# A four-layer graph network in one kernel: the first chunk of its last layer done alone, and the scaling of layer 2's outputs pinned one chunk ahead

## Chip, cores and metric

The kernel runs on one core of a Trainium2 chip. The metric is the device time of one execution in microseconds (us). Engines are named as the profile names them: PE (matrix multiplications, with PEld for its weight loads), DVE (vector), ACT (scalar, activation functions), POOL (general, elementwise here) and SP (issues DMA transfers). Each has a queue of its own and works through it in order; semaphores tie the queues together.

## What is computed

Four graph layers are applied to x, 128 graphs of 64 nodes with 256 features, each with a residual connection: x = x + layer(relu(layernorm(x))). All arithmetic is in fp32. Only the end of layer 2 and layer 3 matter here:

```python
# layer 2
h = relu(batchnorm(agg @ W1.T + b1, g1, be1))      # agg = A_hat @ relu(layernorm(x))
out = batchnorm(h @ W2.T + b2, g2, be2)            # mean and variance over all 8192 tokens
x = x + out
# layer 3
h = relu(layernorm(x))                             # mean and variance over the 256 features of a token
Wh = h @ W
e = leaky_relu(s1[:, :, None] + s2[:, None, :])    # s1 = Wh @ a1, s2 = Wh @ a2
e = where(adj == 0, -inf, e)
x = x + softmax(e) @ Wh
```

The batch normalization that ends layer 2 needs all tokens before the first can be scaled. So layer 3 can start only when layer 2 has been through the last token: there is a seam between the two.

## The kernel before

The 8192 tokens are worked in 16 chunks of 512, a chunk being four token tiles of 128. Layer 2 leaves its raw outputs in SBUF with features on the partitions, `hs[n][0]`, and `fold2.of` (line 1544) turns the collected statistics into a scale and a shift per feature. The residual x of each chunk is loaded by `fetch` (line 1568) into `hs[n][1]` with tokens on the partitions.

Layer 3 then takes each chunk through these steps:

- `second_norm(n)` (line 1572). It makes `o`, the scaled outputs of layer 2, in a buffer of the pool `xin2`, which has four (for chunk 0 one half on DVE, line 1579, and one on ACT, line 1582; for all others both halves on POOL, line 1587). Eight PE transposes with the identity (line 1594) bring it into a pair of PSUM banks, DVE adds it to the residual (line 1596), and takes mean and variance of each of the four token tiles (lines 1600 and 1601). The roots, (variance + 1e-5) to the power -0.5, and the negative product with the mean are four small POOL operations (lines 1603 to 1607). The normalized chunk `h` is four operations of 128x256, on ACT for chunk 0 (line 1615) and on POOL for all others (line 1611).
- `features(n)` (line 1619): eight transposes back (line 1626) and a relu on ACT into `hT` (line 1629).
- `project3(n, tiles)` (line 1635): per token tile two matrix multiplications of 257 columns, copied to `wh` by ACT (line 1650). The multiplications are recorded under the helper's line 50, as are those of the scores and values.
- `dense_scores(n)` (line 1652): the scores, their leaky relu, mask and maximum on DVE (lines 1662 to 1671), exponentials on ACT (line 1674), a reciprocal on DVE (line 1677).
- `turn(n)` (line 1680): four transposes of the exponentials (line 1685), copied by DVE and then ACT into a block-diagonal `field` (line 1689).
- `dense_values(n)` (line 1693): four multiplications, then scale and residual add on DVE (line 1700), and the store of the chunk (line 1708).

The loop at line 1712 writes these out for staggered chunks: in step n, `second_norm(n+2)`, `features(n+1)`, `project3(n)`, `turn(n-1)`, `dense_scores(n)`, `dense_values(n-1)`. This order is only the order of priority. A scheduler fills each engine's queue when the kernel is built, and may put an instruction ahead of earlier ones if it deems its inputs ready sooner. In the built program before, POOL's queue opens layer 3 with ten scalings, those of chunks 1 to 5, ahead of the roots of chunk 0; from then on the scaling of a chunk stands four to five chunks ahead of its use. The helper `late(ins)` (line 71) takes that freedom away: it pins an instruction behind everything written before it for the same engine.

## Time and profile before

| | us |
|---|---|
| median of three runs | 2114.04 |
| lowest and highest of them | 2113.0, 2115.65 |
| the profiled execution: its time | 2112.7 |
| the profiled execution: its span, first to last instruction | 2110.9 |
| last matrix multiplication of layer 2 ends | about 1946.9 |
| first and last transposes L1594 of layer 3 start | 1950.8, 2075.9 |
| last operation on DVE ends, the last store is issued | 2106.7 |

Times inside the profile count from the start of the span. A profile has several views. The totals give each engine's busy time. The view by stretches gives it for parts of the span, with the granted clock of PE (1.00 is full). The chain of waits goes back from the last instruction, at each step to what released it. The timeline lists instructions in order of time. A line such as `h<-pair,h 128x1024` names the tile written and those read.

### The profile page before, as it was taken

What the parts mean: (1) busy time and instruction counts of PE and PEld (TensorE: products, weight loads), DVE (VectorE), ACT (ScalarE), POOL (GpSimd) and SP (SyncE); (2) the same over time, 40 slices, a digit from 0 to 9 for tenths busy, and PEclk for the clock granted to TensorE, in tenths of its full rate; (3) what the DMA queues carried; (4) which work ended last, traced back from release to release, by engine and by line L of the source; (5) the groups of instructions that cost most, each with busy time, mean ns of one, the idle gap of its engine ahead of it and who ended that gap; (6) DMA issues with size and microseconds to landing.
All of it is one profiled execution on the core that took longest, in us unless ns stands there. A gap on an engine that the chain in (4) does not pass through costs nothing.

```text
span 2110.9 us, 25487 instructions
## 1 busy us (share of the span) xinstructions
PE 2028.9 (96%) x9444; PEld 1348.2 (64%) x9444; DVE 1352.1 (64%) x2453; ACT 1186.4 (56%) x2264; POOL 309.1 (15%) x432
## 2 busy tenths in 40 slices
PE   8999999999999999999999998999999989999898
PEld 6776488766688746886668884333334665434686
DVE  8764665564655577556546555576676767786676
ACT  4354766654655467656456554565565356591444
POOL 3000000100200020002001002113312420000662
PEclk9999999999999999999999999999999999999899
DMA  9221000100100340001000006113234751022012
GB/s 315 88 95 50 0 21 1 41 0 1 40 1 1 120 159 20 1 1 40 1 11 30 1 22 203 60 41 104 67 90 131 230 189 60 0 70 90 30 61 70
DMA packets 94444, 135.06 MB, mean 64 GB/s; under 512 B 6384, under 2 KB 82032, under 8 KB 92144
## 3 DMA queue, kind: packets, MB, share of 16 engines
q1 hardware_dynamic: 87600, 109.11, 15.5%
q0 software_dynamic: 6112, 24.12, 3.8%
q8 instruction: 74, 1.21, 0.2%
q10 hardware_dynamic: 608, 0.20, 0.1%
q14 instruction: 50, 0.41, 0.1%
HBM read 87.28 MB, written 46.14 MB: 63 GB/s over the span
## 4 chain that ended last, share of the span: by engine, by line
PE 81%; ACT 6%; DVE 6%; issue 4%; DMA 2%; POOL 1%; SPq 0%; ACTq 0%; POOLq 0%; DVEq 0%
PE pa L641 24%; PE bank L50 20%; PE pc L641 12%; PE pair L50 6%; PE pb L641 6%; PE pa L1341 5%; PE pc L1341 2%; ACT gate L669 2%; PE bank L1132 1%; PE pb L1341 1%; ACT gate L721 1%; PE pair L1626 1%; DMA xo<-xa 1%; PE pair L1594 1%; DVE lstm_c L720 1%
## 5 line engine op out<-in xcount | busy, mean ns | idle before, releaser
L641 PE MATMUL pa<-xop,sih 128*128 128x256 f32 (+2 forms) x1056 | 346.6, 417 | 11.8 <-ACT gate L689 10.1
L669 ACT ACTIVATE gate<-gate,bias 128x256 f32<-128x256 f32 (+2 forms) x368 | 246.9, 678 | 181.0 <-DVE gate L685 97.4
L641 PEld LDWEIGHTS pa<-xop,sih 128*128 128x128 f32 x1056 | 198.5, 190 | 85.5 <-issue 20.9
L641 PE MATMUL pc<-xop,wih 128*128 128x256 f32 (+2 forms) x736 | 251.1, 423 | 0.0
L641 PE MATMUL pa<-lstm_h,shh 128*128 128x256 f32 (+1 forms) x672 | 212.7, 398 | 0.0
L963 DVE SCALAR_TENSOR_TENSOR lr<-lr 128x1024 f32<-128x1024 f32 x128 | 152.0, 1218 | 85.4 <-ACT lr L962 85.2
L685 DVE TENSOR_TENSOR gate<-pb,gate 128x256 f32<-128x256 f32 (+2 forms) x184 | 87.5, 475 | 162.1 <-PE pb L641 126.0
L641 PEld LDWEIGHTS pc<-xop,wih 128*128 128x128 f32 x736 | 139.8, 190 | 51.2 <-issue 22.5
L699 DVE TENSOR_TENSOR gate<-pc,gate 128x256 f32<-128x256 f32 (+2 forms) x184 | 87.4, 475 | 119.2 <-PE pc L641 117.7
L641 PEld LDWEIGHTS pa<-lstm_h,shh 128*128 128x128 f32 x672 | 127.7, 190 | 30.2
L962 ACT COPY lr<-pair 128x1024 f32<-128x1024 f32 x128 | 125.0, 1015 | 34.3 <-PE pair L50 34.3
L641 PE MATMUL pc<-lstm_h,whh 128*128 128x256 f32 (+1 forms) x448 | 141.8, 398 | 0.0
L684 ACT COPY gate<-pa 128x256 f32<-128x256 f32 (+2 forms) x184 | 76.9, 418 | 104.3 <-PE pa L641 103.6
L669 ACT ACTIVATE gate<-pa,bias 128x256 f32<-128x256 f32 (+2 forms) x184 | 94.8, 515 | 71.1 <-PE pa L641 70.1
L50 PE MATMUL pair<-sd_hot,xq 64*128 64x512 f32 x512 | 134.4, 622 | 0.3 <-ACT lr L962 0.3
L50 PE MATMUL bank<-wlv,hT 128*128 128x512 f32 x256 | 122.8, 611 | 7.0 <-ACT hT L154 7.0
L694 DVE TENSOR_TENSOR gate<-pa,gate 128x256 f32<-128x256 f32 (+2 forms) x184 | 87.4, 475 | 35.3 <-PE pa L641 33.1
L641 PE MATMUL pa<-xop,wih 128*128 128x256 f32 (+1 forms) x320 | 101.8, 400 | 5.4 <-ACT xop L622 3.1
L432 POOL TENSOR_TENSOR sih<-wih 128x512 f32<-128x512 f32 x8 | 10.8, 1350 | 632.2 <-DMA wih<-in_WihT 440.7
L641 PE MATMUL pb<-xop,wih 128*128 128x256 f32 (+1 forms) x320 | 100.5, 398 | 0.0
L641 PEld LDWEIGHTS pc<-lstm_h,whh 128*128 128x128 f32 x448 | 85.1, 190 | 20.1
L50 PEld LDWEIGHTS bank<-wlv,hT 128*128 128x128 f32 x256 | 44.8, 189 | 81.9 <-issue 62.1
(321 smaller groups left out, 3844.2 us busy)
## 6 DMA issues: line engine op xcount, KB each, us to landing
field<-sd_hot SPq DMA_DIRECT2D x8, 1152.0 KB, 10.4
wih<-in_WihT SPq DMA_DIRECT2D x8, 1024.0 KB, 5.0
xres<-in_x SPq DMA_DIRECT2D x16, 512.0 KB, 5.3
xa<-xres POOLq DMA_DIRECT2D x16, 512.0 KB, 4.6
xin<-xb SPq DMA_DIRECT2D x16, 512.0 KB, 3.9
h<-xb SPq DMA_DIRECT2D x16, 512.0 KB, 3.8
out_x<-h SPq DMA_DIRECT2D x16, 512.0 KB, 2.9
xin<-in_x SPq DMA_DIRECT2D x15, 512.0 KB, 5.9
```

Source lines behind the costliest of these rows:

```text
L50: nc.tensor.matmul(o, lhsT, rhs, start=start, stop=stop)
L641: ins = nc.tensor.matmul(p[:, : self.N], weights[kind, self.phase](k, q), x[k], start=first_ and kind == "ih", stop=kind == "hh" or not se ...
L669: nc.scalar.activation(out, in_, AF.Tanh if q == 2 else AF.Sigmoid, bias=bias[:, self.w - 1, 2 * q + j : 2 * q + j + 1],)
L684: nc.scalar.copy(blk[0, 0], pa[:, :N])
L685: nc.vector.tensor_tensor(blk[0, 0], pb[:, :N], blk[0, 0], ALU.add)
L694: nc.vector.tensor_tensor(blk[1, 1], pa[:, :N], blk[1, 1], ALU.add)
L699: nc.vector.tensor_tensor(blk[1, 0], pc[:, :N], blk[1, 0], ALU.add)
L720: nc.vector.tensor_tensor(c_, i_, g_, ALU.mult)
L721: nc.scalar.activation(g_, c_, AF.Tanh)
L962: nc.scalar.copy(lr, p)
L963: nc.vector.scalar_tensor_tensor(lr, lr, 0.2, lr, ALU.mult, ALU.max)
L1341: ins = nc.tensor.matmul(p, lhs[k], x[k], start=first_, stop=last_one, skip_group_check=True)
```

## The change

The first chunk gets a function of its own, `first_norm`, which works in two pairs of token tiles: it scales halves of 256 columns on DVE and ACT, adds and normalizes pair by pair, takes its roots with ACT's Sqrt and a reciprocal on DVE, and uses single PSUM banks. Chunk 1 also takes its roots on ACT, and two of its four `h` tiles are made there. The scaling `o` moves out of `second_norm` into `scale_o`, which is pinned with `late` and called for chunk n+3 after `second_norm(n+2)`. Much of chunks 0 to 2 is pinned too. Step 0 of the loop has an order of its own. The store of the last chunk is issued in two halves, the first after its second token tile. PE, DVE and ACT do the same arithmetic on the same sizes otherwise. In the changed file `second_norm`'s transposes are line 1669, its add 1674, its sums 1678 and 1679, the scalings on POOL 1657, the roots on POOL 1688 to 1691, `h` on POOL 1695; in `first_norm` the add is 1602, the root 1609, `h` 1618, the transposes back 1634.

The built program has this order on POOL: scalings of chunks 1 and 2, two `h` tiles of chunk 1, then roots of 2, `h` of 2, scalings of 3, roots of 3, `h` of 3, scalings of 4, and so on in this alternation to chunk 15.

```diff
+        def first_norm():
+            xt, v = xts[0], hs[0][0]
+            o = os3[0]
...
+            for ip in range(2):
+                r = slice(ip * 256, (ip + 1) * 256)
+                late(nc.vector.tensor_scalar(
+                    o[:, 0, r], v[:, 0, r], scale2[:, 0:1], shift2[:, 0:1], ALU.mult, ALU.add
+                ))
+                late(nc.scalar.activation(
+                    o[:, 1, r], v[:, 1, r], AF.Identity, bias=shift2[:, 1:2], scale=scale2[:, 1:2]
+                ))
+            def add(ip):
+                p = bank()
...
+                flat = xt[:, 2 * ip : 2 * ip + 2, :].rearrange("p i d -> p (i d)")
+                late(nc.vector.tensor_tensor(flat, p, flat, ALU.add))
+
+            def sums(ip):
+                i2 = slice(2 * ip, 2 * ip + 2)
+                for i in (2 * ip, 2 * ip + 1):
+                    late(nc.vector.bn_stats(st[:, i, :], xt[:, i, :]))
+                    late(nc.vector.bn_aggr(mv[:, i, :], st[:, i, :]))
+                late(nc.scalar.activation(rs[:, i2], mv[:, i2, 1], AF.Sqrt, bias=eps))
+
+            def root(ip):
+                i2 = slice(2 * ip, 2 * ip + 2)
+                late(nc.vector.reciprocal(rs[:, i2], rs[:, i2]))
+                late(nc.vector.scalar_tensor_tensor(
+                    nm[:, i2], mv[:, i2, 0], -1.0, rs[:, i2], ALU.mult, ALU.mult
+                ))
+                for i in (2 * ip, 2 * ip + 1):
+                    late(nc.scalar.activation(
+                        h[:, i, :], xt[:, i, :], AF.Identity, bias=nm[:, i : i + 1], scale=rs[:, i : i + 1]
+                    ))
+
+            add(0)
+            sums(0)
+            add(1)
+            root(0)
+            sums(1)
+            root(1)
+            yield
...
+        def scale_o(n):
+            half = (0, 1) if n % 2 == 0 else (1, 0)
+            o = os3[n] = xin2.tile([P, 2, CHUNK], F32, tag="xin2", name="o")
+            v = hs[n][0]
+            for c in range(2 if n else 0):
+                late(nc.gpsimd.tensor_scalar(
+                    o[:, c, :], v[:, half[c], :], scale2[:, c : c + 1], shift2[:, c : c + 1], ALU.mult, ALU.add
+                ))
+
         def second_norm(n):
...
-            o = xin2.tile([P, 2, CHUNK], F32, tag="xin2", name="o")
...
-            else:
-                for c in range(2):
-                    nc.gpsimd.tensor_scalar(
-                        o[:, c, :], v[:, half[c], :], scale2[:, c : c + 1], shift2[:, c : c + 1], ALU.mult, ALU.add
-                    )
+            o = os3.pop(n)
...
             rs = stat.tile([P, 4], F32, tag="ln_rs", name="ln_rs")
-            nc.gpsimd.tensor_scalar(rs, mv[:, :, 1], 1e-5, None, ALU.add)
-            nc.gpsimd.tensor_tensor(rs, rs, half_power, ALU.pow)
+            yield
             nm = stat.tile([P, 4], F32, tag="ln_nm", name="ln_nm")
...
+            if n == 1:
+                keep(nc.scalar.activation(rs, mv[:, :, 1], AF.Sqrt, bias=eps))
+                keep(nc.vector.reciprocal(rs, rs))
+                keep(nc.vector.scalar_tensor_tensor(nm, mv[:, :, 0], -1.0, rs, ALU.mult, ALU.mult))
+            else:
+                nc.gpsimd.tensor_scalar(rs, mv[:, :, 1], 1e-5, None, ALU.add)
+                nc.gpsimd.tensor_tensor(rs, rs, half_power, ALU.pow)
...
             for i in range(4):
-                if n:
+                if n > 1 or i > 1:
...
-            nc.sync.dma_start(out=token_tiles(out, n), in_=xt)
+                if n == NCH - 1 and i % 2:
+                    nc.sync.dma_start(
+                        out=token_tiles(out, n)[:, i - 1 : i + 1, :], in_=xt[:, i - 1 : i + 1, :]
+                    )
+            if n < NCH - 1:
+                nc.sync.dma_start(out=token_tiles(out, n), in_=xt)
...
-        for n in range(-2, NCH + 1):
+        for n in range(3):
+            scale_o(n)
+        start = first_norm()
+        next(start)
+        second = second_norm(1)
+        next(second)
+        for _ in start:
+            pass
+        project3(0, (0, 1))
+        for _ in second:
+            pass
+        for n in range(NCH + 1):
             if 4 <= n + 4 < NCH:
                 fetch(n + 4)
             if n + 2 < NCH:
-                second_norm(n + 2)
-            if 0 <= n + 1 < NCH:
+                for _ in second_norm(n + 2):
+                    pass
+            if n + 3 < NCH:
+                scale_o(n + 3)
+            if n == 0:
+                project3(0, (2, 3))
+                dense_scores(0)
+                features(1)
+                continue
+            if n + 1 < NCH:
                 features(n + 1)
```

More of the change, by code (lines that the diff above doesn't have):

```diff
@@ L1570, in fetch @@
             nc.sync.dma_start(out=xts[n], in_=token_tiles(xb[n]))
+        def first_norm():
+            xt, v = xts[0], hs[0][0]
+            o = os3[0]
+            st = stat.tile([P, 4, 6], F32, tag="ln_st", name="ln_st")
+            mv = stat.tile([P, 4, 2], F32, tag="ln_mv", name="ln_mv")
+            rs = stat.tile([P, 4], F32, tag="ln_rs", name="ln_rs")
+            nm = stat.tile([P, 4], F32, tag="ln_nm", name="ln_nm")
+            h = norms[0] = as_tokens(v)
+            hT = t2.tile([P, 2, CHUNK], F32, tag="aggT2", name="hT3")
+            hT3[0] = hT
+            for ip in range(2):
[8 more added lines that the diff above has]
+                p = bank()
+                for i in range(2):
+                    for c in range(2):
+                        k = (2 * ip + i) * P
+                        ins = nc.tensor.transpose(
+                            p[:, (2 * i + c) * P : (2 * i + c + 1) * P], o[:, c, k : k + P], ident
+                        )
+                        if i + c == 0:
+                            late(ins)
+                flat = xt[:, 2 * ip : 2 * ip + 2, :].rearrange("p i d -> p (i d)")
[23 more added lines that the diff above has]
+            yield
+            norms.pop(0)
+            for ip in range(2):
+                p = bank()
+                for i in range(2):
+                    for c in range(2):
+                        ins = nc.tensor.transpose(
+                            p[:, (2 * i + c) * P : (2 * i + c + 1) * P],
+                            h[:, 2 * ip + i, c * P : (c + 1) * P],
+                            ident,
+                        )
+                        if i + c == 0:
+                            late(ins)
+                late(nc.scalar.activation(
+                    hT[:, :, ip * 256 : (ip + 1) * 256].rearrange("p c (i t) -> p i c t", i=2),
+                    p.rearrange("p (i c t) -> p i c t", i=2, c=2),
+                    AF.Relu,
+                ))
+                yield
@@ L1572, in second_norm @@
+        os3 = {}
+        def scale_o(n):
[5 more added lines that the diff above has]
+                    o[:, c, :], v[:, half[c], :], scale2[:, c : c + 1], shift2[:, c : c + 1], ALU.mult, ALU.add
+                ))
         def second_norm(n):
             xt, v = xts[n], hs[n][0]
-            half = (0, 1) if n % 2 == 0 else (1, 0)
@@ L1577, in second_norm @@
-            o = xin2.tile([P, 2, CHUNK], F32, tag="xin2", name="o")
-            if n == 0:
-                nc.vector.tensor_scalar(
-                    o[:, 0, :], v[:, half[0], :], scale2[:, 0:1], shift2[:, 0:1], ALU.mult, ALU.add
-                )
-                nc.scalar.activation(
-                    o[:, 1, :], v[:, half[1], :], AF.Identity, bias=shift2[:, 1:2], scale=scale2[:, 1:2]
-                )
-            else:
-                for c in range(2):
-                    nc.gpsimd.tensor_scalar(
-                        o[:, c, :], v[:, half[c], :], scale2[:, c : c + 1], shift2[:, c : c + 1], ALU.mult, ALU.add
-                    )
+            o = os3.pop(n)
@@ L1593, in second_norm @@
                     k = (i % 2 * 2 + c) * P
-                    nc.tensor.transpose(p[:, i // 2, k : k + P], o[:, c, i * P : (i + 1) * P], ident)
+                    ins = nc.tensor.transpose(p[:, i // 2, k : k + P], o[:, c, i * P : (i + 1) * P], ident)
+                    if n < 3 and i + c == 0:
+                        late(ins)
             flat = xt.rearrange("p i d -> p (i d)")
-            nc.vector.tensor_tensor(flat, p.rearrange("p b d -> p (b d)"), flat, ALU.add)
+            keep = late if n < 3 else lambda ins: ins
+            keep(nc.vector.tensor_tensor(flat, p.rearrange("p b d -> p (b d)"), flat, ALU.add))
             st = stat.tile([P, 4, 6], F32, tag="ln_st", name="ln_st")
@@ L1599, in second_norm @@
             for i in range(4):
-                nc.vector.bn_stats(st[:, i, :], xt[:, i, :])
-                nc.vector.bn_aggr(mv[:, i, :], st[:, i, :])
+                keep(nc.vector.bn_stats(st[:, i, :], xt[:, i, :]))
+                keep(nc.vector.bn_aggr(mv[:, i, :], st[:, i, :]))
             rs = stat.tile([P, 4], F32, tag="ln_rs", name="ln_rs")
-            nc.gpsimd.tensor_scalar(rs, mv[:, :, 1], 1e-5, None, ALU.add)
-            nc.gpsimd.tensor_tensor(rs, rs, half_power, ALU.pow)
+            yield
             nm = stat.tile([P, 4], F32, tag="ln_nm", name="ln_nm")
-            nc.gpsimd.tensor_tensor(nm, mv[:, :, 0], rs, ALU.mult)
-            nc.gpsimd.tensor_scalar(nm, nm, -1.0, None, ALU.mult)
+            if n == 1:
[5 more added lines that the diff above has]
+                nc.gpsimd.tensor_tensor(rs, rs, half_power, ALU.pow)
+                nc.gpsimd.tensor_tensor(nm, mv[:, :, 0], rs, ALU.mult)
+                nc.gpsimd.tensor_scalar(nm, nm, -1.0, None, ALU.mult)
             h = norms[n] = as_tokens(v)
             for i in range(4):
-                if n:
+                if n > 1 or i > 1:
                     nc.gpsimd.tensor_scalar(
@@ L1707, in dense_values @@
                 )
-            nc.sync.dma_start(out=token_tiles(out, n), in_=xt)
+                if n == NCH - 1 and i % 2:
+                    nc.sync.dma_start(
+                        out=token_tiles(out, n)[:, i - 1 : i + 1, :], in_=xt[:, i - 1 : i + 1, :]
+                    )
+            if n < NCH - 1:
+                nc.sync.dma_start(out=token_tiles(out, n), in_=xt)
         for n in range(4):
             fetch(n)
-        for n in range(-2, NCH + 1):
+        for n in range(3):
[10 more added lines that the diff above has]
+        for n in range(NCH + 1):
             if 4 <= n + 4 < NCH:
```

## The prediction

> **What bounds the kernel now.** I read the engines' totals first, then the busy time by stage, the chain of waits from the end of layer 2 on, a steady stretch of layer 3 in order of time, and last the granted TensorE clock.

> ```profile
> PE 2028.9 (96%) x9444; PEld 1348.2 (64%) x9444; DVE 1352.1 (64%) x2453; ACT 1186.4 (56%) x2264; POOL 309.1 (15%) x432
> ```
> ```profile
> 1946.00:1972.00 26.00, 15.87 (x78) 12.49 (x77) 14.11 (x42) 6.75 (x14) 18.68 (x32) 0.67 0.08 27
> ...
> 1980.00:2077.00 97.00, 97.00 (x588) 78.77 (x587) 75.59 (x216) 47.68 (x169) 59.11 (x105) 1.00 0.18 61
> ```
> The columns are the stretch, its length, the busy time of PE, PEld, DVE, ACT and POOL, then the clock. Layer 3 has three parts. From 1980 to 2077 PE never rests: the bound is PE, 8.61 us a chunk (the transposes L1594 of two successive chunks start at 2032.89 and 2041.50). From 1946 to 1972 PE is busy 15.9 of 26 us at two thirds of its clock. The end, after 2094, is the last chunk alone. Nothing before 1950 is touched.

> ```profile
> 1950.35 1.07 POOL o L1587
> ...
> 1952.16 2.82 POOL o L1587 x4
> ...
> 1955.16 3.02 POOL o L1587 x4
> ...
> 1958.27 0.24 POOL ln_rs L1603
> ...
> 1958.59 1.05 POOL ln_rs L1604
> ...
> 1960.27 0.61 ACT h L1615
> ...
> 1960.92 2.17 PE pair L1626 x8
> ```
> The start is held by POOL: ten scalings of five chunks stand ahead of the roots of chunk 0, so the normalized chunk 0 appears only at 1960.27.

> ```profile
> 2032.89 1.04 PE L1594 MATMUL pair<-ident,o 128*128 128x128 f32 x8
> ...
> 2034.24 1.52 POOL L1587 TENSOR_SCALAR o<-h,scale,shift 128x512 f32<-128x512 f32 x2
> ...
> 2034.86 1.21 DVE L1596 TENSOR_TENSOR h<-pair,h 128x1024 f32<-128x1024 f32 x1
> ...
> 2037.94 0.17 DVE L1601 BATCH_NORM_AGGREGATE ln_mv<-ln_st 128x2 f32<-128x6 f32 x1
> ...
> 2038.20 0.23 POOL L1603 TENSOR_SCALAR ln_rs<-ln_mv 128x4 f32<-128x4 f32 x1 [2.44 <-DVE ln_mv L1601]
> ...
> 2040.26 2.61 POOL L1611 TENSOR_SCALAR h<-h,ln_rs,ln_nm 128x256 f32<-128x256 f32 x4
> ...
> 2041.50 1.04 PE L1594 MATMUL pair<-ident,o 128*128 128x128 f32 x8
> ```
> One chunk passes L1594 on PE, the add and the sums on DVE, the roots and h on POOL. That takes longer than 8.61 us, but costs nothing, because o for the next L1594 was made four chunks earlier.

> ```profile
> 1273.10:1276.51 3.41, 1.56 (x8) 1.03 (x6) 2.62 (x4) 1.80 (x3) 0.00 (x0) 1.00 0.76 240
> ...
> 1945.53:1948.94 3.41, 1.33 (x4) 0.26 (x2) 2.98 (x5) 0.29 (x1) 0.00 (x0) 1.00 0.46 152
> 1948.94:1952.35 3.41, 1.36 (x5) 1.07 (x6) 1.61 (x8) 1.11 (x2) 2.00 (x3) 0.50 0.28 99
> 1962.59:1966.01 3.42, 3.42 (x18) 3.42 (x17) 1.18 (x1) 1.09 (x2) 3.08 (x6) 0.50 0.00 0
> ```
> A stretch of 3.41 us with PE busy 1.33 us was followed by half clock; one with 1.56 us was not. The clock came back after a full stretch.

> [...] the drops at 1279.93 and 1948.94 lie 669.0 us apart, 196 windows. [...] The trace has one load, 1.28 us at 1974.30, before the first exp. The three new Sqrts precede that exp, so no load is added.

> **The change part by part.** Chunk numbers are in brackets. Queue orders are those of the changed program as built.

> First chunk. DVE and ACT scale halves from 1950.2. The transposes of pair 0 end at 1951.8. The add of 128x512 is taken at 0.69 us (as L1361) and ends at 1952.54. Sums now stand strictly in order, 0.54 us a tile (0.39 + 0.16, against the 0.4 of a mixed order), so to 1953.6. Sqrt 0.29 (as L1312), the second add, reciprocal and product: h of tile 0 starts at 1954.7, which is 5.6 us earlier. Pair 1 has h at 1957.66. The projection of chunk 0 starts at 1958.3 instead of 1966.16. Its two single PSUM banks in place of a pair cost nothing: all four are free then. POOL is rid of the roots of [0] and [1] (2.0 us each) and of two h tiles of [1], which is worth nothing by itself, since what it does next waits for scores and sums.

> What takes that lead away. PE is at half clock until a full window ends at 1962.6, so projecting the first two token tiles takes 8 x 0.44 = 3.5 us. The Sqrt of [1] stands on ACT behind two wh copies, which wait for these projections: 1962.45. Behind it are h [1] on ACT and POOL (to 1964.3), then scores [0] to 1965.9, features [1] to 1966.7 and half of projection [1] to 1969.3. The sums of [2] are interleaved on DVE with the score operations of [0], so the roots of [2] start at 1967.65, h runs from 1969.7 to 1972.0, and only then comes o [3], to 1973.55. PE idles some 4.2 us for it, and loses the clock at 1972.83 until 1976.25. PE then reaches the end of values [0] at 1981.65, where it was at 1981.25 before: the 7.8 us are gone. And o [4] still has to pass the add of [3] (1975.5), its sums (to 1978.8), 2.06 us of roots, 2.6 of h, 1.55 of o: ready at 1985.1. **Start: 1985.1 - 1981.25 = +3.8 us.**

> The loop. scale_o(n+3) is pinned behind the POOL operations of second_norm(n+2). So o[k+1] waits for h[k], and h[k] for L1594[k] (now L1669), which waits for o[k]. Queued behind the waiting transpose on PE is everything else, and ACT and DVE wait for that. From "o[k] ready", with the rows above:
> - transposes: 0.05 + 7 x 0.109 + 0.16 until visible + 0.04 = 1.01
> - add 1.21: 2.22
> - sums, with the field copy ahead of the last aggregate as in the trace. That copy needs turn on PE: 0.81 + 6 x 0.218 + 0.87 + 0.44 + 0.44, visible at 4.03; copy 0.39; aggregate: 4.55
> - semaphore 0.08, roots to h 2.06 (2038.20 to 2040.26), h 2.59, o 1.52: 10.80

> **10.80 against 8.61, over the 11 steps from [4] to [15]: +24.1 us.** Without the field copy's wait it is 10.6; with h at the 2.2 us of an undisturbed stretch, 10.2. No sum comes below 8.61: POOL's 6.2 alone plus 1.0, 1.2 and 1.6 is 10.0.

> The clock in the loop. PE idles about 2.15 us in each step, near the limit between 1.85 (3.41 - 1.56) and 2.08 (3.41 - 1.33). With 1.95 it drops when the idle time lies in one window, in 49% of phases. A step without a drop moves the phase by 10.80 - 3 x 3.413 = 0.56, one with a drop by 2.26; followed from 1985.1, that gives 4 drops in 11. A drop halves one window of work ahead of turn: 1.7 us. **4 x 1.7 = +6.8 us**; bounds 0 and 18.7.

> The end. The add of [15] no longer waits for the reciprocal L1677 (0.9 us in before): -0.9. The store in halves adds one issue of 0.37 us on SP, with only the second half behind it. 256 KB should land between the 2.4 us of a 128 KB load and the 2.9 of 512 KB: -0.3 (0 to -0.5).

> Sum: 3.8 + 24.1 + 6.8 - 0.9 - 0.3 = +33.5 us. The profiled execution took 2112.7 (span 2110.9 and 1.8 around it): 2146.2. The median of the runs lies 1.3 above it, so 2147.

> **Rivals.**
> - No drops in the loop, or a shorter chain. 33.5 - 6.8 = +26.7 gives 2141; with 10.2 us a step (11 x 1.6 instead of 24.1) 2134. For it: idle 2.15 is at the limit.
> - A drop in nearly every step: 11 x 1.7 = 18.7 instead of 6.8 gives 2159. For it: at the limit a small delay more is enough.
> - Faster. One mechanism decides: the circle o, L1669, sums, roots, h, o is shorter than PE's 8.61 us. Then only the 5.6 us of the first chunk and the 1.2 at the end count: 2107. Against it stand the 10.0 us above; POOL would have to run its 6.2 us in under 4.8.
> - The change doesn't reorder POOL: excluded by the built order, where o[k+1] follows h[k] from [2] on.

> **How the numbers follow.** Forecast (2 to 6 drops) 0.55, no drops or a shorter chain 0.23, a drop in nearly every step 0.16, faster 0.04, a balance near zero 0.02. The range from 2133 to 2159 takes in the first two and most of the third. A measurement can tell about 0.2%, 4 us: slower 0.94, same 0.02, faster 0.04.

> **What would show it.** h of chunk 0 (L1618) at about 1954.7; one gap of PE near 1969 to 1973; L1669 of successive chunks 10.6 to 12.5 us apart, each released by POOL o; POOL with no idle time but the wait for ln_mv; half clock in several slices of the last 150 us. I am wrong if successive L1669 stand 8.6 us apart, or if the half clock fails to come or stays.

## The result, and the profile after

The changed kernel takes 2147.74 us (median of 5 runs, 2147.47 to 2153.67) against 2114.04 us before (5 runs, 2113.0 to 2118.51). The ratio is 1.0158, with a 95% interval of 1.0147 to 1.0169: 33.7 us slower by the medians, where 2147 us was forecast. The profiled execution has a span of 2145.7 us instead of 2110.9.

The totals of the changed kernel's page:

```profile
PE 2047.7 (95%) x9444; PEld 1357.0 (63%) x9444; DVE 1355.3 (63%) x2461; ACT 1187.8 (55%) x2270; POOL 303.9 (14%) x422
```

Its view by stretches, over the steady part of layer 3 (columns as in the prediction):

```profile
1982.00:2128.00 146.00, 123.24 (x669) 94.47 (x669) 86.45 (x239) 55.38 (x195) 71.53 (x125) 0.95 0.14 48
```

The totals hide it: PE is at 95% instead of 96%, and POOL is the least busy engine by far. The stretch shows it: PE, which was busy for all of 97 us before, rests for 22.8 of 146 us and has 0.95 of its clock. POOL is busy for 71.5 of the 146. At 49% it holds up everything, since its work stands in a circle with that of others. The chain of waits of the changed kernel gives this circle; one step of it, from one o to the next:

```profile
2042.24 1.51 POOL o L1657 x2
...
2043.79 0.99 PE pair L1669 x7
2044.78 1.30 PE bank L50 x6
2046.08 0.87 PE pair L1710 x8
2046.96 0.43 PE bank L50 x2
2047.39 0.45 PE bank L1769 x4
...
2047.87 0.42 DVE field L1773
2048.28 0.10 DVE ln_mv L1679
...
2048.46 0.24 POOL ln_rs L1688
...
2050.51 2.57 POOL h L1695 x4
2053.08 1.51 POOL o L1657 x2
```

The step is 10.84 us. More than half of it is POOL's own (1.51, 2.57 and 2.05 for the roots), the rest passes over PE and DVE, and the aggregate L1679 stands on DVE behind the field copy L1773, as in the prediction's working. The timeline shows the other side, PE waiting for POOL (in brackets the idle time before, and what ended it):

```profile
2043.04 0.33 PE L1669 MATMUL pair<-ident,o 128*128 128x128 f32 x1 [1.38 <-POOL o L1657]
...
2043.79 0.99 PE L1669 MATMUL pair<-ident,o 128*128 128x128 f32 x7 [0.42 <-POOL o L1657]
```

From [4] to [15], "o ready" to "o ready", the eleven steps are 11.00, 12.61, 10.84, 12.51, 10.84, 10.85, 12.52, 10.84, 10.84, 12.52 and 10.84 us. The four long ones hold a stretch at half clock. The trace of this execution records PE's clock in 26 stretches, each at 1.00 or 0.50; all but the last, in which the profile ends, are 3.41 us long or a whole multiple of that (from one to 160 times 3.413). A piece of this grid of 3.41 us is called a window here. Stretches as long as one window show one of the four and one step that keeps its clock. Their edges lie about 0.15 us later than those of this execution's windows, which is why they read 0.98 and 0.52 and not 1.00 and 0.50:

```profile
2018.41:2021.83 3.42, 1.72 (x11) 1.48 (x12) 2.12 (x6) 1.44 (x8) 1.97 (x3) 0.98 0.24 81
2021.83:2025.24 3.41, 3.41 (x14) 2.93 (x13) 2.47 (x8) 0.38 (x1) 0.00 (x0) 0.52 0.22 73
...
2042.31:2045.72 3.41, 2.26 (x14) 1.93 (x15) 2.11 (x5) 0.98 (x7) 1.43 (x2) 1.00 0.40 135
```

The stretch with PE busy for 1.72 us is followed by one at half clock, the stretch with 2.26 is not. With edges 0.15 us earlier, on the windows themselves, the two are 1.62 and 2.10 us. Before the three other drops of the loop it was 1.46, 1.62 and 1.62 us; the least in the loop that kept the clock was 1.88. PE's rest in a step is 1.80 us (1.38 + 0.42), and a window that takes in all of it has 3.41 - 1.80 = 1.61 us of work left: in this loop the four windows that hold a whole wait for o are the four that a window at half clock followed; where the wait lay over two windows, each had 1.88 us or more and the clock stayed. A limit in busy time for all kinds of work does not follow. In the start of the same execution a window with 1.87 us (1956.82 to 1960.23), mostly transposes, was followed by half clock.

Where the 34.8 us of span went:

| part | us |
|---|---|
| layer 3 begins later (L1318, which completes the shift of the batch normalization on DVE, at 1952.25 instead of 1950.02) | +2.2 |
| from there until o of chunk 4, o [4], is ready: 33.7, where it was 31.2 to L1594 [4] | +2.5 |
| 11 steps: 126.2 instead of 94.7 | +31.5 |
| from o [15] ready to the end: 33.55 instead of 34.99 (there from L1594 [15]) | -1.4 |

The first row is not the change's. It arises in parts that the diff doesn't touch, and one of the experiments below, the same as the kernel before up to the last store, began layer 3 at 1952.49. Over the nine profiled executions of this case L1318 starts between 1949.7 and 1954.3.

### The profile page after: what moved, and what is told of

The parts are those of the page before. It is cut to its first block, busy times and chain, and to the rows that moved or that the text cites. A ratio compares the mean times of both kernels' runs of the same rounds, so it can differ in the third digit from the quotient of the medians.

```text
span 2145.7 us, 25492 instructions
## 1 busy us (share of the span) xinstructions
PE 2047.7 (95%) x9444; PEld 1357.0 (63%) x9444; DVE 1355.3 (63%) x2461; ACT 1187.8 (55%) x2270; POOL 303.9 (14%) x422
## 3 DMA queue, kind: packets, MB, share of 16 engines
q8 instruction: 74, 1.21, 0.2%
## 4 chain that ended last, share of the span: by engine, by line
PE 82%; ACT 5%; issue 4%; POOL 4%; DVE 3%; DMA 1%; ACTq 0%; DVEq 0%; POOLq 0%; SPq 0%
PE pa L641 24%; PE bank L50 20%; PE pc L641 12%; PE pb L641 6%; PE pair L50 5%; PE pa L1341 5%; PE bank L1132 3%; PE pc L1341 2%; ACT gate L669 2%; POOL h L1695 2%; PE pb L1341 1%; ACT gate L721 1%; PE pair L1112 1%; POOL o L1657 1%; PE pair L1669 1%
## 5 line engine op out<-in xcount | busy, mean ns | idle before, releaser
L641 PE MATMUL pa<-xop,sih 128*128 128x256 f32 (+2 forms) x1056 | 347.4, 418 | 10.3 <-ACT gate L689 8.6
L962 ACT COPY lr<-pair 128x1024 f32<-128x1024 f32 x128 | 124.9, 1015 | 34.3 <-PE pair L50 31.2
L432 POOL TENSOR_TENSOR sih<-wih 128x512 f32<-128x512 f32 x8 | 10.6, 1320 | 631.5 <-PE pa L641 263.9
```

Of the source, the lines that this page charges most:

```text
L641: ins = nc.tensor.matmul(p[:, : self.N], weights[kind, self.phase](k, q), x[k], start=first_ and kind == "ih", stop=kind == "hh" or not se ...
L962: nc.scalar.copy(lr, p)
```

## The experiments

The theory is that of the prediction: the pin of the scalings closes a circle o, transposes, add and sums, roots, h, next o of 10.8 us, and PE's rest in it costs the clock in four of the eleven steps. The rivals: the loss comes from the new first chunk or the roots moved to ScalarE; or it comes from the order of POOL's work in general and not from how far ahead o is made. In all experiments the kernel before ran beside them on the same chip, at 2115.34 us for the first four and, on another chip, at 2116.13 us for the last three. Times of different groups are therefore compared by their distance from it.

### The pin alone

```diff
+        def scale_o(n):
...
-                    nc.gpsimd.tensor_scalar(
+                    (late if n > 2 else lambda ins: ins)(nc.gpsimd.tensor_scalar(
...
             if n + 2 < NCH:
                 second_norm(n + 2)
+            if 3 <= n + 3 < NCH:
+                scale_o(n + 3)
```

The kernel before, with only this; scale_o takes the scalings out of second_norm.

> The kernel before, with only the scalings of chunks 3 to 15 pinned behind the POOL operations of the chunk ahead; first chunk, roots and store as before. Theory 1 (circle through POOL): steps of 10.85 us, 12.5 where the clock drops, 11 of them, and a start some 3 us late: about 2149 us. Theory 2 (first chunk, ACT roots or step 0): within 2 us of the kernel before, 2114 us.

Measured: 2154.64 us, ratio 1.0182 (1.0165 to 1.0199). The chain of waits of this kernel has the same circle, here in its lines from one o to the next and on into a stretch at half clock:

```profile
2035.66 1.51 POOL o L1587 x2
...
2038.19 1.31 PE bank L50 x6
...
2046.50 1.51 POOL o L1587 x2
...
2049.03 2.36 PE bank L50 x6
```

From one o to the next it is again 10.84 us, and the same six multiplications take 2.36 us instead of 1.31 where the clock is halved. The steps from the add of [5] on are 11.69, 12.52, 10.84, 10.84, 12.52, 10.88, 10.84, 12.52, 10.84, 10.84 us. The loop, from the add of [4] to that of [15], takes 125.6 us, where the whole change takes 126.2. So the pin alone gives all of the loss in the loop. The time is 39.3 us above the kernel before, some 6 us more than with the whole change and 4 us more than expected. The difference lies outside the loop: from L1318 to the add of [4] it is 37.6 us instead of 34.8, and from the add of [15] to the end 36.5 instead of 32.5. The rest of the change is a gain.

### The change without the pin

```diff
-                late(nc.gpsimd.tensor_scalar(
+                (late if n < 3 else lambda ins: ins)(nc.gpsimd.tensor_scalar(
```

> The changed kernel with the pin taken off the scalings of chunks 3 to 15 alone; the built program then puts the scalings of chunks 1 to 5 first on POOL, as the kernel before did. Theory 1 (circle through POOL): 8.61 us a step, about 2108 us, the same as with the scaling called earlier. Theory 2 (first chunks, ACT roots or step 0 are the cause): about 2147 us. If ten scalings at the front hurt chunk 1, whose h stands behind them on POOL, it is 1 to 3 us above the kernel that calls the scaling earlier.

Measured: 2111.63 us, ratio 0.9983 (0.9975 to 0.9992), faster than before. The steps are 8.61 us. POOL's timeline in this kernel is instructive:

```profile
2002.62 0.23 POOL L1688 TENSOR_SCALAR ln_rs<-ln_mv 128x4 f32<-128x4 f32 x1 [2.45 <-DVE ln_mv L1679]
...
2004.67 2.57 POOL L1695 TENSOR_SCALAR h<-h,ln_rs,ln_nm 128x256 f32<-128x256 f32 x4
2007.22 1.51 POOL L1657 TENSOR_SCALAR o<-h,scale,shift 128x512 f32<-128x512 f32 x2
```

The order on POOL is the same, roots, h, o, and so are the durations. POOL waits for the sums here too. What differs is whose o it is: one for several chunks later, so that nobody waits for it. The rival that blames POOL's order in general is out; it is the distance that counts.

### The pin kept, the scaling one place earlier

```diff
+            if n + 3 < NCH:
+                scale_o(n + 3)
             if n + 2 < NCH:
                 for _ in second_norm(n + 2):
                     pass
-            if n + 3 < NCH:
-                scale_o(n + 3)
```

> The changed kernel with scale_o(n+3) called ahead of second_norm(n+2), so that on POOL the scaling of chunk k+1 stands ahead of the roots and h of chunk k. Theory 1 (the circle o, L1669, sums, roots, h, o on POOL sets the step): the circle is open, L1669 of successive chunks stand 8.61 us apart again, no half clock after about 1970, and what is left are the gains of start and end, about 4.8 and 1.4 us: 2108 us. Theory 2 (the steady loop is slowed by the pinned order of the first chunks, by ACT's roots, or by the new order of step 0): about 2147 us, steps of 10.85 us as in the changed kernel.

Measured: 2112.01 us, ratio 0.9983 (0.9976 to 0.9990), steps of 8.61 us. The pin as such costs nothing here, and a lead of one chunk is enough, if o [k+1] is not behind the roots of [k].

The timeline shows the lead: an o that is made right after an h, and the transposes 8.61 us apart, of which the first shown takes this o 5.7 us after it is ready.

```profile
1999.78 0.56 POOL L1695 TENSOR_SCALAR h<-h,ln_rs,ln_nm 128x256 f32<-128x256 f32 x1
...
2000.32 1.52 POOL L1657 TENSOR_SCALAR o<-h,scale,shift 128x512 f32<-128x512 f32 x2
...
2007.58 1.03 PE L1669 MATMUL pair<-ident,o 128*128 128x128 f32 x8
...
2016.19 1.04 PE L1669 MATMUL pair<-ident,o 128*128 128x128 f32 x8
```

The time is that of the change without the pin within 0.4 us, so the ten scalings in front, which that kernel has, cost chunk 1 nothing that can be seen. In both kernels the circle is gone, but the gain is about 3.5 us and not the 7 expected. The transposes L1669 of [4] start 29.5 and 29.6 us after L1318, where they started 31.2 after it before: the start has gained 1.6 to 1.7 us and not 4.8. Why is tested in the last experiment.

### Half of h on ScalarE

```diff
-                if n > 1 or i > 1:
+                if i > 1:
                     nc.gpsimd.tensor_scalar(
...
                 else:
                     nc.scalar.activation(
```

> The changed kernel with two of the four h tiles of every chunk from 2 on made by ACT instead of POOL. Theory 1: the circle loses two POOL operations of 0.65 us, so a step is 10.85 - 1.3 = 9.55 us; PE then idles 0.9 us a step, too little for the clock to drop: 11 x 0.94 = 10.3 us over the kernel before in the loop, 2124 us in all. Theory 2 (the step is set elsewhere): 2147 us or more, as ACT gets longer.

Measured: 2135.15 us, ratio 1.0089 (1.0072 to 1.0106). The direction is right, and the size is missed: 19.8 us above the kernel before, where 10.3 was expected. The steps repeat 9.5, 11.0, 10.7, 10.4: only one in four has the length that POOL's shortened chain gives. The chain of waits of this kernel shows what comes in:

```profile
2023.01 1.09 ACT h L1699 x2
2024.10 0.27 ACT wh L1734
...
2024.39 0.43 DVE e L1746
...
2026.93 1.18 DVE h L1784 x3
2028.10 1.13 DVE h L1674
```

The two tiles of h stand on ACT ahead of a copy of wh, the scores on DVE wait for that copy, and the add L1674 of the next chunk stands on DVE behind the scores and behind L1784. The last seven of its transposes ran on PE from 2025.99 to 2026.97, and DVE comes to it only at 2028.10. The work taken from the circle on POOL put a second circle, over ACT and DVE, in its place. That the clock would hold was foreseen rightly: PE's rest is shorter, no window of the loop has less than about 1.8 us of its work (windows placed by the pace of PE's multiplications at the start of this execution), and none is at half clock: eight transposes L1710 take 1.03 to 1.06 us in every step.

### Spare work for PE in the wait

```diff
             p = pair_bank()
+            for j in range(8 if n > 2 else 0):
+                late(nc.tensor.transpose(p[:, j // 4, j % 4 * P : (j % 4 + 1) * P], ident, ident))
             for i in range(4):
```

> The changed kernel with eight spare transposes of ident (0.87 us of PE at full clock) ahead of the transposes of o for every chunk from 3 on; they need no o, so they run in the wait for it, and the idle time of PE in a step falls from about 2.15 us to about 1.3 us. Theory (the four steps of 12.5 us are those in whose 3.41 us window PE's idle time of 2.15 us lies whole): no window falls under 1.6 us of PE work, the clock stays full, all steps are 10.85 us, and the time is 2147.7 - 4 x 1.67 = 2141.0. Rival (the clock follows something other than PE's idle time, or the long steps come from another wait): four steps of 12.5 remain and the time is 2147.7 or above.

Measured: 2136.01 us (2131.15 to 2138.94), ratio 1.009 (1.0073 to 1.0107). In its stretches of one window's length, PE is never busy for less than 2.92 us from 1991 to 2119, and the clock stays at 1.00, here around one wait:

```profile
2045.72:2049.13 3.41, 2.99 (x18) 2.41 (x18) 3.25 (x7) 0.93 (x6) 3.32 (x5) 1.00 0.00 0
```

No step of 12.5 us is left. But the experiment did a second thing: the steps are 10.22 us and not 10.85, because the scheduler, given more work for PE, also placed the field copy on DVE behind the last aggregate of the sums instead of ahead of it. One step of its chain of waits:

```profile
2050.11 1.23 DVE h L1676
...
2052.91 0.23 DVE ln_mv L1681 x2
...
2055.26 2.33 POOL h L1697 x4
2057.60 1.67 POOL o L1657 x2
```

PE's projections, the turn and the field copy no longer stand in it: from the start of the add to the end of the last aggregate it is 3.0 us where it was 3.6, h is 0.24 us shorter and o 0.16 longer. Over the loop, from the add of [4] to that of [15], 112.8 us instead of 126.2: four drops of 1.67 are 6.7 of the 13.4, eleven times 0.62 are 6.8. Of the span 10.7 us are saved: the 13.4, less 1.4 at the start and 1.3 at the end, where the last chunk has a window at half clock. Against the kernel beside it the time is 19.9 us longer, with the change it was 33.7.

The drops go when PE rests less, here and in the kernel with half of h on ScalarE, which has no spare work. This experiment doesn't tell the spare work from the shorter step, since both take from the rest: a step of 10.22 us without spare work would leave PE about 1.80 - 0.62 = 1.2 us of it (an estimate), less than the 1.53 (3.41 - 1.88) that kept the clock in the changed kernel.

### The last store alone

```diff
-            nc.sync.dma_start(out=token_tiles(out, n), in_=xt)
+                if n == NCH - 1 and i % 2:
+                    nc.sync.dma_start(
+                        out=token_tiles(out, n)[:, i - 1 : i + 1, :], in_=xt[:, i - 1 : i + 1, :]
+                    )
+            if n < NCH - 1:
+                nc.sync.dma_start(out=token_tiles(out, n), in_=xt)
```

The kernel before, with only this.

> The kernel before, with the last store issued in two halves and nothing else changed. Theory (a half lands sooner than the whole): from the end of the last DVE operation to the end of the span 3.5 us instead of 4.2, and a time 0.7 us lower, less than the timing can tell. Rival (the shorter tail seen in the changed kernel came from the other changes): 4.2 us stays.

Measured: 2115.68 us, ratio 0.9998 (0.9989 to 1.0006), the same within the measurement. In the profiles the last DVE operation (1.66 us, from 2109.14) ends at 2110.8, and the span at 2114.3: 3.5 us, against 4.3 before. The gain of the halves is 0.8 us and belongs to them.

### Keeping the clock at the start

```diff
             def add(ip):
                 p = bank()
+                for j in range(0 if ip else 26):
+                    late(nc.tensor.transpose(p[:, j % 4 * P : (j % 4 + 1) * P], ident, ident))
```

It takes the change without the pin, and puts in the same way 16 spare transposes ahead of the transposes of o [1], 10 ahead of those of h [0] and 14 ahead of those of h [2], whose first transpose is pinned behind them.

> The changed kernel without the pin from chunk 3 on (as in the run without the pin), with spare transposes of ident in PE's waits at the start of layer 3: 26 ahead of the first transposes of o [0], 16 ahead of those of o [1], 10 ahead of the transposes of h [0], 14 ahead of those of h [2]. Theory (the half clock takes away the lead of the first chunk): the clock stays full from 1947 to 1980, the projection of chunk 0 takes 1.75 us instead of 3.37, the transposes of h [2] and the projection behind them 2.2 us instead of 4.9, and the time is 3 to 4 us below the run without the pin, about 2108. Rival (the chain of sums, roots and h of chunk 2 on DVE and POOL holds the start, whatever PE's clock): the same time as without the pin, 2111.6, within 1 us.

Measured: 2109.66 us (2106.84 to 2110.24), ratio 0.9971 (0.9959 to 0.9982), the fastest of all. By the ratios that is 0.12% or 2.5 us below the change without the pin; the theory had 3 to 4. The intervals of the two ratios overlap, so it is the traces that show what the clock did. Two stretches of 3.41 us at the start of the kernel without the spare transposes, each in part at half clock:

```profile
1956.97:1960.39 3.42, 2.40 (x8) 1.70 (x9) 3.21 (x9) 2.17 (x4) 1.70 (x3) 0.69 0.00 0
...
1970.62:1974.04 3.42, 3.14 (x11) 2.30 (x12) 0.45 (x4) 1.53 (x5) 3.25 (x7) 0.70 0.00 0
```

Stretches at nearly the same times in the kernel with them, which reads 1.00 in every stretch of 3.41 us from 1936 to 1997:

```profile
1956.73:1960.14 3.41, 2.92 (x14) 2.18 (x15) 2.87 (x9) 2.29 (x5) 1.14 (x2) 1.00 0.00 0
...
1970.38:1973.79 3.41, 3.41 (x21) 2.65 (x21) 0.42 (x1) 2.35 (x7) 2.97 (x7) 1.00 0.00 0
```

The first chunk's projection is multiplied at full clock, in 2.0 us instead of 3.4, and L1669 of [4] (L1675 here) starts 26.6 us after L1318 instead of 29.6. The transposes of h [2] and the projection behind them take 3.4 us, not the 2.2 expected, since the transposes wait for h on POOL. So about half of the 5.6 us that the first chunk was to gain was lost to the clock, as the prediction's working of the start had it. The rival, that the chain of chunk 2 over DVE and POOL sets the start whatever the clock, is refuted for these 3 us.

## Why the prediction was right, step by step

The time fell 0.7 us from the forecast, and the mechanism is the one forecast. The terms of its sum are not all equally right.

- **The start, +3.8: measured +2.5.** Set against the 2.2 us by which layer 3 begins later, h of chunk 0 starts at 1954.4 (forecast 1954.7), the Sqrt of [1] at 1961.9 (1962.45), the roots of [2] at 1966.7 (1967.65), PE's gap before L1669 [3] is 2.9 us (4.2). The chain is right, and the roots of [2] are 1 us earlier than worked out. The clock's windows lay otherwise to the work than in the execution before: L1318 starts 2.26 us after the edge at 1949.99, where it started 1.08 us after the one at 1948.94, which was not in the forecast. The new Sqrts on ACT added no ACT_TABLE_LOAD, as forecast: both traces have seven of 1.28 us, one of them in layer 3, ahead of its first exp (1969.61; before at 1974.30).
- **The loop, 11 x (10.80 - 8.61) = +24.1: measured 10.84 a step without a drop, +24.6.** The parts agree one by one: field copy ready 4.09 us after o (forecast 4.03), sums done at 4.63 (4.55), h begins at 6.76 (6.69), h 2.57 (2.59), o 1.51 (1.52). Using h of the loop, 2.6, and not the 2.2 of an undisturbed stretch was right: in the start of the same profile, for [2] from 1971.09 and with DVE idle, it is 2.17. In the loop the four operations of an h have different lengths: in that from 2050.51 on, 0.80 us for the one beside L1752 and 0.71 for the one beside L1753 on DVE, and 0.55 for the other two, as for all four at 1971.09. No run here separates what makes the two longer.
- **The clock, 4 x 1.7 = +6.8: measured 4 x 1.67 = 6.7.** The number is right, the two figures behind it are not. The forecast took 2.15 us of rest in a step and a limit between 1.85 and 2.08. In the trace the rest is 1.38 + 0.42 = 1.80 us, since the first transpose needs only the first half of o and runs between. And in the loop rests of 1.79 to 1.95 us in a window (3.41 - 1.62 and 3.41 - 1.46) were followed by half clock, while 1.53 (3.41 - 1.88) was not. Rest and limit were both too high, and the errors cancelled; that it came out at exactly four owes something to luck. What does hold is the way it was counted, by the phase of the steps to windows of 3.41 us.
- **The end, -0.9 and -0.3: measured -1.4 in all.** From the last DVE operation to the end it is 3.5 us instead of 4.3, so the halves are worth 0.8, beyond the bound of 0.5, and 0.6 is left for the add where 0.9 was expected. The bound for 256 KB was put between the times of a smaller load and of a whole store; the half that ends the kernel gains more, and why stays open.
- **What the prediction didn't have: +2.2** from the later beginning of layer 3. It lies in the spread of single executions. The sum without it would be 32.6, 0.9 below the 33.5 that were forecast. That the median came within 0.7 us is closer than terms that miss by up to 2.2 us can promise.

Of the rivals, "no drops" fell in the changed kernel because the four drops are in its trace; the windows show how near it was, since after a rest shorter by 0.3 us (1.53) the clock stayed. "Faster" needed a circle under 8.61 us. The kernel with the scaling one place earlier shows what it would have given: 3.3 us below the kernel before and not 7, since the 5.6 us of the first chunk were taken at face value there, while the working of the start had already shown them eaten by the clock. That price of the rival contradicted the forecast's own reasoning.

## What to carry to other kernels

Before pinning or moving a producer in an engine's queue, write down the circle: what it waits for, and whether that waits, by way of other engines, for what it made last. If the circle is longer than the step of the bounding engine, the loss is the difference times the steps (here 11 x (10.84 - 8.61) us, with POOL busy 49% of the time), however idle the engine looks; here one chunk of lead, taken ahead of the waiting instruction, removed it (steps of 8.61 us). And when the bounding engine begins to rest, count its clock too: put the rest beside the windows in its record (3.41 us here), and try spare work in it (here eight transposes a chunk, with which it stayed at 1.00).
